# A graph-network layer on one core: node features loaded first in three transfers per 2048 nodes, and the stores of h on GpSimd's queue

## The chip, the core and the metric

The kernel runs on one core of a Trainium2 chip. A core has a matrix engine (TensorE, PE in the profile), a vector engine (VectorE, DVE), a scalar engine (ScalarE, ACT), GpSimd (POOL) and a small engine that issues transfers (SyncE, SP). Each engine works through its own list of instructions in order; semaphores order the engines among each other. Transfers (DMAs) are issued by SP, ACT or POOL and are carried out by 16 DMA engines that all three share. In the profile SPq and ACTq are the issuing side of SP and ACT, and POOLq that of GpSimd; transfers issued by SP and ACT show up under "hardware_dynamic" queues, GpSimd's under "software_dynamic".

The metric is device time in microseconds (us). The kernel before takes 4074.11 us (median of 10 runs, 4069.6 to 4077.16).

## The reference

12,500 nodes with 160 features each (64 scalars and 32 vectors of 3), 400,000 edges sorted by their destination. What matters here, with the constant factors left out:

```
s = x[:, :64];  v = x[:, 64:].reshape(n, 32, 3);  a = node_attr
h_s = s @ lin1_ws * a                      # the table h: 12500 x 160
h_v = einsum('nci,cd->ndi', v, lin1_wv) * a
w   = silu(edge_scalars @ fc_w1) @ fc_w2   # 224 weights for each edge, in five parts w1..w5
es, ev = h_s[edge_src], h_v[edge_src]      # one row of h gathered for each edge
m_s1 = w1 * es * e0;   m_s2 = w4 * (ev . e1);   m_v1 = w2 * es x e1
m_v2 = w3 * ev * e0;   m_v3 = w5 * cross(ev, e1)
agg_s, agg_v = segment_sum(..., edge_dst)
out = layernorm(x + gate(self_connection(x) + agg @ lin2))
```

## The kernel before

**The opening (lines 98 to 396).** Everything from line 95 to line 396 is kept in the order in which it is written, on each engine. It has to leave three things behind: the table h in memory (`h_tab`, 12,500 rows of 640 bytes), a small integer for each edge (`rel`: its destination less the base of its block of three tiles), and the scaled weights.

The table is made in pieces of 2048 nodes (CH, six of them, and a rest of 212). For each piece SP loads the features channel by channel: `xa` (128 x 2048: 64 scalars and the first two components of the 32 vectors) in four transfers (lines 274 and 275, 1024 nodes each), and `xz` (the third component, the piece cut in four quarters that lie under each other, 128 x 512) in four (line 279). All seven pieces have buffers of their own (`nodes`, bufs = 7), so that no load waits for a buffer. PE multiplies 16 tiles of 128 nodes by `l1` (line 316) and the four of `xz` by the block-diagonal `l1z` (line 331). DVE scales the results by the node attribute while it moves them from PSUM to `ht` (lines 319 and 334, five instructions of 128 x 512 for each piece). `ht` has three buffers. ACT then stores the piece (line 345, 128 partitions x 16 rows of 640 bytes, 2048 rows in all), and the rest as one tile of 128 rows and one of 84 (line 348).

Before that, SP loads `rows`, the first destination of each block, straight from `dst` in three transfers of single elements (lines 254 and 255); `bases()` (line 292, called ahead of the fourth piece) turns it into `lo`, the bases spread over 128 partitions, and the flag `early`. After the pieces SP loads the first indices (`idx`), edge attributes (`eat`), edge scalars (`es`, line 228, two halves of 64 x 1536), `w1` and, in ten transfers, `w2` with its columns rearranged (line 289); ACT loads `dt`, all destinations (line 351, 128 x 3125 integers), behind the stores. DVE then scales `w2`, makes `rel` from `dt` and `lo` (lines 387 and 392, 17 instructions) and scales the second layer's weights `l2` (line 111), which SP loads in 20 small transfers (line 380).

**The loop over the edges (from line 785).** 782 steps of four tiles of 128 edges. A step gathers with four indirect transfers on GpSimd's queue (line 427, 128 rows of h each; `hg` has four buffers of four tiles, so GpSimd can be 16 gathers ahead), makes the edge weights on PE (lines 418 and 440), the products of both on DVE (lines 450 and 458, which read `hg`), a selection matrix from `rel` on DVE (lines 504 and 507), sums tiles into blocks on PE (line 514), and adds blocks into an accumulator. The nodes that are complete are finished along the way.

**How transfers are counted.** The framework gives each transfer one of eight semaphores in turn. SP and ACT share one set of eight; GpSimd has eight of its own. A transfer is only issued once the earlier transfer on its semaphore has landed, so that a load on SP can wait for a store that ACT issued.

Of the kernel before, what the change touches and what calls it, by code (L numbers as in the profile page):

```python
# [10 lines left out]
F32 = mybir.dt.float32  # L11
# [9 lines left out]
P = 128  # L21
S = 64
V = 32
# [5 lines left out]
BT = 3  # L29
# [3 lines left out]
KB = 4  # L33
# [7 lines left out]
NWT = 224  # L41
# [12 lines left out]
def gnn_kernel(  # L54
# [21 lines left out]
    nc = tc.nc  # L76
    N = x.shape[0]
    NT = attr.shape[1]
# [4 lines left out]
    NB = -(-TT // BT)  # L83
# [3 lines left out]
    consts = ctx.enter_context(tc.tile_pool(name="consts", bufs=1))  # L87
    dram = ctx.enter_context(tc.tile_pool(name="dram", bufs=1, space=bass.MemoryType.DRAM))
    h_tab = dram.tile([N, D], F32, name="h_tab")
# [5 lines left out]
    in_order = ctx.enter_context(ExitStack())  # L95
    in_order.enter_context(tc.manual_schedule(
        engines={ENG.PE, ENG.DVE, ENG.Activation, ENG.Pool, ENG.SP}))
    at = consts.tile([P, NT], F32, name="at")
    nc.scalar.dma_start(at, attr)

    l1 = consts.tile([P, P], F32, name="l1")
    nc.vector.memset(l1, 0.0)
    nc.scalar.dma_start(l1[:S, :S], lin1_ws)
    for i in range(2):
        r = slice(S + i * V, S + (i + 1) * V)
        nc.scalar.dma_start(l1[r, r], lin1_wv)
    scales = [(l1[:S], 1.0 / math.sqrt(S)), (l1[S:], 1.0 / math.sqrt(V))]

    def scale():
        for m, by in scales:  # L110
            nc.vector.tensor_scalar_mul(m, m, by)
        scales.clear()

    def block_diagonal(name, w, n, scale, queue=nc.scalar):
        k = w.shape[0]
        m = consts.tile([n * k, n * k], F32, name=name)
        nc.vector.memset(m, 0.0)
        for i in range(n):
            queue.dma_start(m[i * k:(i + 1) * k, i * k:(i + 1) * k], w)
        if scale != 1.0:  # L120
            scales.append((m, scale))
        return m

    l1z = block_diagonal("l1z", lin1_wv, 4, 1.0 / math.sqrt(V))
    for m, by in scales:
        nc.scalar.mul(m, m, by)
    scales.clear()


    rel = consts.tile([P, TT], I16, name="rel")  # L130
    rows = consts.tile([1, NB], I32, name="rows")
    early = consts.tile([1, 1], F32, name="early")
# [8 lines left out]
    ends_pool = ends.enter_context(tc.tile_pool(name="ends", bufs=1))  # L141
# [49 lines left out]
    def index(t):  # L191
        a0, idx, _ = ahead(t)
        return idx[:, t - a0:t - a0 + 1]
# [20 lines left out]
    def in_pairs(a):  # L214

        return a.rearrange("o (c k h) -> o h c k", k=KB, h=2)

    ess = {}

    def load_chunk(c):  # L220
        if c in ess:
            return
        t0, halves = chunks[c]
        es = ess[c] = loads.tile([2 * S, SIDE * P], F32, name="es")
        for half, n in enumerate(halves):
            to = es[half * S:(half + 1) * S]
            e0 = (t0 + half * halves[0]) * P
            nc.sync.dma_start(to[:, :n * P], es_t[:, e0:e0 + n * P])


    ident = consts.tile([P, P], F32, name="ident")
# [16 lines left out]
                   base=0, channel_multiplier=0)  # L248
    nc.gpsimd.iota(share[:, even:], pattern=[[RATE, NB - even]], base=even * RATE, channel_multiplier=0)

    with nc.allow_non_contiguous_dma(reason="the first destination of each block"):
        firsts = dst[0:1, 0:(even - 1) * BT + 1:BT].rearrange("o (c h k) -> o h c k", k=KB, h=2)
        for half in range(2):
            nc.sync.dma_start(in_pairs(rows[:, :even])[:, half], firsts[:, half])
        nc.sync.dma_start(rows[:, even:], dst[0:1, even * BT:(NB - 1) * BT + 1:BT])


    U = 4
    dt = ends_pool.tile([P, TT], I32, name="dt")
    lo = ends_pool.tile([P, NB], F32, name="lo")  # L260
# [2 lines left out]
    with tc.tile_pool(name="nodes", bufs=len(starts)) as nodes, tc.tile_pool(  # L263
        name="nodes_ps", bufs=6, space=PSUM
    ) as nps, tc.tile_pool(name="z_ps", bufs=2, space=PSUM) as zps:
        loaded = []
        for c0 in starts:
            cn = min(CH, N - c0)
            quarters = 4 if cn == CH else 1
            assert quarters == 4 or cn <= U * P  # L270
            xa = nodes.tile([P, CH], F32, name="xa")
            for b0 in range(0, cn, CH // 2):
                b1 = min(b0 + CH // 2, cn)
                nc.sync.dma_start(xa[:S, b0:b1], xs_t[:, c0 + b0:c0 + b1])
                nc.sync.dma_start(xa[S:, b0:b1], xv_t[:2 * V, c0 + b0:c0 + b1])
            xz = nodes.tile([P, U * P], F32, name="xz")
            cq = cn // quarters
            for q in range(quarters):
                nc.sync.dma_start(xz[q * V:(q + 1) * V, :cq],
                                  xv_t[2 * V:, c0 + q * cq:c0 + (q + 1) * cq])  # L280
            loaded.append((c0, cn, quarters, cq, xa, xz))
        index(0)
        load_chunk(0)
        for half in range(2):
            r = slice(half * S, (half + 1) * S)
            nc.sync.dma_start(w1[r, r], fc_w1)
            at_c = 0
            for a, b in ((64, 128), (0, 64), (192, 224), (160, 192), (128, 160)):
                nc.sync.dma_start(w2[r, half, at_c:at_c + b - a], fc_w2[:, a:b])
                at_c += b - a  # L290

        def bases():

            base_f = ends_pool.tile([1, NB], F32, name="base_f")
            nc.vector.tensor_copy(base_f, rows)
            for b0 in range(0, NB, U * P):
                b1 = min(NB, b0 + U * P)
                ps = nps.tile([P, U, P], F32, name="hp").rearrange("p u c -> p (u c)")
                nc.tensor.matmul(ps[:, :b1 - b0], ones, base_f[:, b0:b1], start=True, stop=True)
                nc.scalar.copy(lo[:, b0:b1], ps[:, :b1 - b0])  # L300
            nc.vector.tensor_sub(share, rows, share)
            nc.vector.tensor_reduce(early, share, AX.X, OP.min)
            nc.vector.tensor_scalar(early, early, -float(MARGIN), None, op0=OP.is_lt)

        for c0, cn, quarters, cq, xa, xz in loaded:
            if c0 == 3 * CH:
                bases()
            ht = nodes.tile([P, 4 * U, D], F32, name="ht", bufs=3)
            nt = -(-cn // P)
            first = c0 // P  # L310
            full = cn // P
            for t0 in range(0, nt, U):
                ps = nps.tile([P, U, P], F32, name="hp")
                for t in range(t0, min(t0 + U, nt)):
                    n = min(P, cn - t * P)
                    nc.tensor.matmul(ps[:n, t - t0], xa[:, t * P:t * P + n], l1,
                                     start=True, stop=True)
                k = min(U, full - t0)
                nc.vector.tensor_mul(
                    ht[:, t0:t0 + k, :P], ps[:, :k],  # L320
                    at[:, first + t0:first + t0 + k, None].to_broadcast([P, k, P]))
                if t0 + k < nt <= t0 + U:
                    n = cn - full * P
                    nc.vector.tensor_scalar(ht[:n, full, :P], ps[:n, full - t0],
                                            at[:n, first + full:first + full + 1], None, op0=OP.mult)

            pz = zps.tile([P, U, 4, V], F32, name="pz")
            k = quarters * V
            for u in range(-(-cq // P)):
                n = min(P, cq - u * P)  # L330
                nc.tensor.matmul(pz[:n, u, :quarters].rearrange("p q c -> p (q c)"),
                                 xz[:k, u * P:u * P + n], l1z[:k, :k], start=True, stop=True)
            if quarters == 4:
                nc.vector.tensor_mul(
                    ht[:, :, P:].rearrange("p (q u) c -> p u q c", q=4), pz,
                    at[:, first:first + 4 * U].rearrange("p (q u) -> p u q", q=4)[:, :, :, None]
                    .to_broadcast([P, U, 4, V]))
            else:
                nc.vector.tensor_mul(ht[:, :full, P:], pz[:, :full, 0],
                                     at[:, first:first + full, None].to_broadcast([P, full, V]))  # L340
            if cn > full * P:
                n = cn - full * P
                nc.vector.tensor_scalar(ht[:n, full, P:], pz[:n, full, 0],
                                        at[:n, first + full:first + full + 1], None, op0=OP.mult)
            nc.scalar.dma_start(
                h_tab[c0:c0 + full * P, :].rearrange("(q p) d -> p q d", p=P), ht[:, :full])
            if cn > full * P:
                nc.scalar.dma_start(h_tab[c0 + full * P:c0 + cn, :], ht[:n, full])


    nc.scalar.dma_start(dt, dst)
    iota = consts.tile([P, W], F32, name="iota")
    nc.vector.tensor_copy(iota, iota_i)
    nc.vector.tensor_scalar_mul(w2, w2, 1.0 / math.sqrt(64))

    scs = consts.tile([S, V3], F32, name="scs")
    nc.sync.dma_start(scs, sc_ws)
# [606 lines left out]
```

## Time and profile before

| | |
|---|---|
| median of 10 runs | 4074.11 us (4069.6 to 4077.16) |
| the profiled execution, its own time | 4064.87 us |
| its span (first to last instruction) | 4063.1 us |
| PE busy | 3692.2 us, 91% |
| POOL busy | 3007.1 us, 74% |
| DVE busy | 2432.4 us, 60% |
| ACT busy | 939.0 us, 23% |
| bytes moved | 411.77 MB, mean 101 GB/s; 209 GB/s in the first of 40 slices |

The profiled execution lies 9.2 us (0.2%) below the median of the runs. The span is what the trace covers; the remaining 1.8 us lie around it. Busy counts the time in which an engine executes: issuing a transfer is not counted on SP and ACT, but GpSimd's part in an indirect transfer is (line 427). Matmuls are pipelined, so that a PE at 91% is not known to be at its limit. In what follows a line of the timeline reads: start, duration, engine, line of the kernel, operation, output <- input, count, and in brackets the idle time of the engine before it with what ended it ("issue" is a wait that the profile does not explain).

### The profile page before, as it was taken

Reading aid. Unit: us, or ns where it says so; the run is one execution under the profiler, and the core shown is the slowest. Engines: PE = TensorE matmul, PEld = TensorE weight load, DVE = VectorE, ACT = ScalarE, POOL = GpSimd, SP = SyncE. Lnnn points to the kernel's source line nnn. Section 1 sums busy time; section 2 is a strip of 40 time slices with the busy share of each in tenths; the row PEclk is TensorE's granted clock in tenths of the full one; section 3 lists DMA queues with packets and bytes.
Section 4 is the critical chain, followed back from the end, with each engine's and each line's share of the span. In section 5 each row is a group of like instructions: output and inputs, shape, how many; then the busy total and the mean of one; then the engine's idle time right before and its main releaser. Section 6 shows DMA issues by size and latency. Waiting matters only on the chain. (4 is left out here: it accounts for less than half of the span.)

```text
span 4063.1 us, 47627 instructions
## 1 busy us (share of the span) xinstructions
PE 3692.2 (91%) x14291; PEld 1600.9 (39%) x14291; DVE 2432.4 (60%) x6374; ACT 939.0 (23%) x2463; POOL 3007.1 (74%) x3134
## 2 busy tenths in 40 slices
PE   5999998998999989998998989999998999998997
PEld 4343343443433433433433434334343333333443
DVE  4665665665656656656656556565665655655655
ACT  0322221221222222212212122122221221221222
POOL 2777777777777777777777777777777777777775
PEclk7999999999999999999999999999999999999998
DMA  7434444434434434434444344444443443443432
GB/s 209 115 91 101 101 97 102 101 95 104 100 91 108 100 90 108 103 92 107 98 100 100 94 97 108 96 98 103 98 105 94 101 104 94 101 101 97 99 95 57
DMA packets 241211, 411.77 MB, mean 101 GB/s; under 512 B 74200, under 2 KB 171876, under 8 KB 240820
## 3 DMA queue, kind: packets, MB, share of 16 engines
q0 software_dynamic: 150000, 256.20, 26.2%
q1 hardware_dynamic: 77666, 142.75, 14.7%
q10 hardware_dynamic: 13282, 9.69, 0.8%
q8 instruction: 119, 1.95, 0.2%
q14 instruction: 144, 1.18, 0.1%
HBM read 392.40 MB, written 16.00 MB: 101 GB/s over the span
## 5 line engine op out<-in xcount | busy, mean ns | idle before, releaser
L427 POOL DMA_INDIRECT hg<-h_tab,idx x3125 | 3002.3, 961 | 1023.3 <-issue 935.9
L440 PE MATMUL pw<-w,hid 128*128 128x448 f32 x3126 | 1383.9, 567 | 199.9 <-DVE oh L504 191.8
L450 DVE TENSOR_TENSOR pr<-pw,hg 128x512 f32<-128x512 f32 x782 | 539.6, 690 | 1471.0 <-DMA hg<-h_tab,idx 1020.5
L514 PE MATMUL pa<-pr,sel 128*64 128x416 f32 x6250 | 1305.0, 539 | 0.0
L458 DVE TENSOR_TENSOR pr<-pw,hg 128x384 f32<-128x384 f32 x2346 | 1153.5, 546 | 0.1
L440 PEld LDWEIGHTS pw<-w,hid 128*128 128x128 f32 x3126 | 561.0, 196 | 691.8 <-issue 624.8
L514 PEld LDWEIGHTS pa<-pr,sel 128*64 128x64 f32 x6250 | 388.2, 139 | 817.0 <-issue 699.5
L706 ACT COPY sa<-pa 128x416 f32<-128x416 f32 x521 | 263.1, 505 | 1474.0 <-PE pa L514 1471.3
L418 PE MATMUL ph<-es,w 128*128 128x512 f32 (+1 forms) x784 | 453.0, 660 | 16.8 <-DMA w<-in_fc_w_dram 11.7
L420 ACT ACTIVATE hid<-ph 128x512 f32<-128x512 f32 x392 | 233.5, 596 | 734.4 <-PE ph L418 733.9
L523 PEld LDWEIGHTS pt<-ident,sa 128*128 128x128 f32 x2084 | 239.9, 141 | 312.1 <-issue 255.0
L507 DVE TENSOR_TENSOR sel<-oh,eas 128x256 f32<-128x256 f32 x782 | 336.9, 431 | 42.8
L538 PE MATMUL po<-tt,l 128*96 128x256 f32 (+5 forms) x1496 | 346.6, 379 | 4.0 <-DVE z L573 2.6
L523 PE MATMUL pt<-ident,sa 128*128 128x128 f32 x2084 | 328.3, 280 | 2.9 <-DVE acc L687 2.5
L538 PEld LDWEIGHTS po<-tt,l 128*96 128x96 f32 (+1 forms) x1496 | 227.8, 163 | 143.2 <-issue 74.0
L526 ACT COPY tt<-pt 128x192 f32<-128x192 f32 x521 | 164.5, 316 | 506.2 <-PE pt L523 505.7
L418 PEld LDWEIGHTS ph<-es,w 128*128 128x128 f32 x784 | 119.7, 192 | 285.0 <-issue 227.2
L546 DVE TENSOR_TENSOR acc<-acc,os 96x32 f32 x1042 | 193.7, 186 | 24.6 <-ACT os L541 5.4
L504 DVE TENSOR_TENSOR oh<-rel,iota 128x64 f32<-128x64 int16 x782 | 169.5, 217 | 0.1
L572 PE MATMUL pp<-ident,acc 96*128 96x96 f32 x196 | 36.6, 273 | 93.6 <-DVE acc L546 73.4
L528 ACT COPY tt<-pt 128x64 f32<-128x64 f32 x521 | 117.1, 225 | 0.0
L541 ACT COPY os<-po 96x512 f32<-96x512 f32 (+2 forms) x68 | 38.3, 563 | 308.4 <-PE po L538 292.3
(77 smaller groups left out, 630.6 us busy)
## 6 DMA issues: line engine op xcount, KB each, us to landing
es<-in_es_t_dram SPq DMA_DIRECT2D x260, 384.0 KB
hg<-h_tab,idx POOLq DMA_INDIRECT x3125
h_tab<-ht ACTq DMA_DIRECT2D x6, 1280.0 KB
xt<-in_x_dram SPq DMA_DIRECT2D x23, 320.0 KB
out_dram<-y SPq DMA_DIRECT2D x23, 320.0 KB
xv<-in_xv_t_dram SPq DMA_DIRECT2D x25, 187.5 KB
xs<-in_xs_t_dram SPq DMA_DIRECT2D x25, 125.0 KB
xa<-in_xs_t_dram SPq DMA_DIRECT2D x12, 256.0 KB
```

What stands on the lines that cost most here:

```text
L418: nc.tensor.matmul(ph[:k, c], w1[:k, :k], es[:k, t0 * P + c0 * P:t0 * P + c1 * P], start=True, stop=True)
L420: nc.scalar.activation(hid[:k, c], ph[:k, c], AF.Silu, scale=1.0 / math.sqrt(64))
L427: nc.gpsimd.indirect_dma_start(out=hg[:, t, :], out_offset=None, in_=h_tab, in_offset=bass.IndirectOffsetOnAxis(ap=i, axis=0))
L440: nc.tensor.matmul(pw[:, t:t + m, :NWT], hid[:m * S, c * P:(c + 1) * P], w2[:m * S, :m], start=True, stop=True)
L450: nc.vector.tensor_mul(two, pw[:, :n, :2 * S].rearrange("p t (k c) -> p t k c", k=2), hg[:, :n, None, :S].to_broadcast([P, n, 2, S]))
L458: nc.vector.tensor_mul(pr[:, :n, first:first + V3].rearrange("p t (i c) -> p t i c", i=3), pw[:, :n, None, 2 * S + k * V:2 * S + (k + 1) * ...
L507: nc.vector.tensor_mul(sel[:, :n], oh[:, :, None, :].to_broadcast([P, n, 4, W]), by_slot(tiles[0][0])[:, u:u + n, :, None].to_broadcast([P ...
L514: nc.tensor.matmul(pa[half * ROWS:(half + 1) * ROWS, :NPR], sel[:, t].rearrange("p k w -> p (k w)"), pr, start=start, stop=stop)
L523: nc.tensor.transpose(pt[:, four * P:four * P + k], sa[:k, c:c + P], ident[:k, :k])
L538: nc.tensor.matmul(po[:, k, :nb], l2[r, terms[to, part, four]], a[:, :nb], start=(n == 0), stop=(n == len(of) - 1))
L546: nc.vector.tensor_add(window, window, os[:, :, b])
L706: nc.scalar.copy(sa, pas.pop(j)[:, :NPR])
```

## The change

SP's first instructions are now the loads of the first piece; a piece takes three transfers (`xs`, `xv`, and all four quarters of `xz` in one, with the rows in the order channel by quarter, so that `l1z` is filled with a step of four partitions). The first destinations come from one row of `dst` that ACT loads into the first partition of `dt`, from where DVE copies `rows` (three copies in `bases()`). The stores of h, the first two halves of edge scalars and the destinations `dt` are issued by GpSimd, in this order, ahead of the first gather; the store of the last 84 rows goes to SP. `fc_w2` is loaded whole in two transfers (`raw`), and DVE rearranges it while it scales it (ten instructions for one).

```diff
-    with nc.allow_non_contiguous_dma(reason="the first destination of each block"):
-        firsts = dst[0:1, 0:(even - 1) * BT + 1:BT].rearrange("o (c h k) -> o h c k", k=KB, h=2)
-        for half in range(2):
-            nc.sync.dma_start(in_pairs(rows[:, :even])[:, half], firsts[:, half])
-        nc.sync.dma_start(rows[:, even:], dst[0:1, even * BT:(NB - 1) * BT + 1:BT])
...
-        for c0 in starts:
+        def load(c0):
...
-            for b0 in range(0, cn, CH // 2):
-                b1 = min(b0 + CH // 2, cn)
-                nc.sync.dma_start(xa[:S, b0:b1], xs_t[:, c0 + b0:c0 + b1])
-                nc.sync.dma_start(xa[S:, b0:b1], xv_t[:2 * V, c0 + b0:c0 + b1])
+            nc.sync.dma_start(xa[:S, :cn], xs_t[:, c0:c0 + cn])
+            nc.sync.dma_start(xa[S:, :cn], xv_t[:2 * V, c0:c0 + cn])
             xz = nodes.tile([P, U * P], F32, name="xz")
             cq = cn // quarters
-            for q in range(quarters):
-                nc.sync.dma_start(xz[q * V:(q + 1) * V, :cq],
-                                  xv_t[2 * V:, c0 + q * cq:c0 + (q + 1) * cq])
+            z = xv_t[2 * V:, c0:c0 + cq]
+            if quarters == 4:
+                nc.sync.dma_start(xz[:, :cq], bass.AP(tensor=z.tensor, offset=z.offset,
+                                                      ap=[[z.ap[0][0], V], [cq, 4], [1, cq]]))
+            else:
+                nc.sync.dma_start(xz[S:S + V, :cq], z)
...
+        load(starts[0])
+        at = consts.tile([P, NT], F32, name="at")
+        nc.scalar.dma_start(at, attr)
...
+        l1z = consts.tile([P, P], F32, name="l1z")
+        nc.vector.memset(l1z, 0.0)
+        for q in range(4):
+            nc.scalar.dma_start(l1z[q:q + 4 * V - 3:4, q * V:(q + 1) * V], lin1_wv)
...
+        nc.scalar.dma_start(dt[0:1], dst[0:1])
+        for c0 in starts[1:]:
+            load(c0)
         index(0)
-        load_chunk(0)
+        raw = ends_pool.tile([2 * S, NWT], F32, name="raw")
         for half in range(2):
             r = slice(half * S, (half + 1) * S)
             nc.sync.dma_start(w1[r, r], fc_w1)
-            at_c = 0
-            for a, b in ((64, 128), (0, 64), (192, 224), (160, 192), (128, 160)):
-                nc.sync.dma_start(w2[r, half, at_c:at_c + b - a], fc_w2[:, a:b])
-                at_c += b - a
+            nc.sync.dma_start(raw[r], fc_w2)
 
         def bases():
 
+            firsts = dt[0:1, 0:(even - 1) * BT + 1:BT].rearrange("o (c h k) -> o h c k", k=KB, h=2)
+            for half in range(2):
+                nc.vector.tensor_copy(in_pairs(rows[:, :even])[:, half], firsts[:, half])
+            nc.vector.tensor_copy(rows[:, even:], dt[0:1, even * BT:(NB - 1) * BT + 1:BT])
...
-            nc.scalar.dma_start(
+            nc.gpsimd.dma_start(
                 h_tab[c0:c0 + full * P, :].rearrange("(q p) d -> p q d", p=P), ht[:, :full])
             if cn > full * P:
-                nc.scalar.dma_start(h_tab[c0 + full * P:c0 + cn, :], ht[:n, full])
-
-
-    nc.scalar.dma_start(dt, dst)
+                nc.sync.dma_start(h_tab[c0 + full * P:c0 + cn, :], ht[:n, full])
+
+
+    load_chunk(0, nc.gpsimd)
+    nc.gpsimd.dma_start(dt, dst)
...
-    nc.vector.tensor_scalar_mul(w2, w2, 1.0 / math.sqrt(64))
+    for half in range(2):
+        r = slice(half * S, (half + 1) * S)
+        at_c = 0
+        for a, b in ((64, 128), (0, 64), (192, 224), (160, 192), (128, 160)):
+            nc.vector.tensor_scalar_mul(w2[r, half, at_c:at_c + b - a], raw[r, a:b], 1.0 / math.sqrt(64))
+            at_c += b - a
```

The definitions of `at`, `l1`, `scale` and `block_diagonal` move behind `load(starts[0])` unchanged; `load_chunk` gets its queue as an argument. In the order of instructions of the changed program two things move with it: SP issues the store of the last 84 rows behind five loads of the edge loop (`xs`, `xv` of the self-connection, `idx`, `eat`), and the 20 scalings of `l2` on DVE, which in the program before lie between the products of the first three steps, come ahead of the first product.

More of the change, by code (lines that the diff above doesn't have):

```diff
@@ L97, in gnn_kernel @@
         engines={ENG.PE, ENG.DVE, ENG.Activation, ENG.Pool, ENG.SP}))
[L98 to L127, printed above, removed]
     rel = consts.tile([P, TT], I16, name="rel")
@@ L218, in gnn_kernel, with load_chunk @@
     ess = {}
-    def load_chunk(c):
+    def load_chunk(c, queue=nc.sync):
         if c in ess:
@@ L227, in load_chunk @@
             e0 = (t0 + half * halves[0]) * P
-            nc.sync.dma_start(to[:, :n * P], es_t[:, e0:e0 + n * P])
+            queue.dma_start(to[:, :n * P], es_t[:, e0:e0 + n * P])
     ident = consts.tile([P, P], F32, name="ident")
@@ new lines, in gnn_kernel, with scale @@
+        nc.scalar.dma_start(at, attr)
+        l1 = consts.tile([P, P], F32, name="l1")
+        nc.vector.memset(l1, 0.0)
+        nc.scalar.dma_start(l1[:S, :S], lin1_ws)
+        for i in range(2):
+            r = slice(S + i * V, S + (i + 1) * V)
+            nc.scalar.dma_start(l1[r, r], lin1_wv)
+        scales = [(l1[:S], 1.0 / math.sqrt(S)), (l1[S:], 1.0 / math.sqrt(V))]
+        def scale():
+            for m, by in scales:
+                nc.vector.tensor_scalar_mul(m, m, by)
+            scales.clear()
@@ new lines, in block_diagonal @@
+        def block_diagonal(name, w, n, scale, queue=nc.scalar):
+            k = w.shape[0]
+            m = consts.tile([n * k, n * k], F32, name=name)
+            nc.vector.memset(m, 0.0)
+            for i in range(n):
+                queue.dma_start(m[i * k:(i + 1) * k, i * k:(i + 1) * k], w)
+            if scale != 1.0:
+                scales.append((m, scale))
+            return m
+        l1z = consts.tile([P, P], F32, name="l1z")
+        nc.vector.memset(l1z, 0.0)
+        for q in range(4):
+            nc.scalar.dma_start(l1z[q:q + 4 * V - 3:4, q * V:(q + 1) * V], lin1_wv)
@@ L282, in gnn_kernel @@
+        scales.append((l1z, 1.0 / math.sqrt(V)))
+        for m, by in scales:
+            nc.scalar.mul(m, m, by)
+        scales.clear()
+        nc.scalar.dma_start(dt[0:1], dst[0:1])
+        for c0 in starts[1:]:
+            load(c0)
         index(0)
-        load_chunk(0)
+        raw = ends_pool.tile([2 * S, NWT], F32, name="raw")
         for half in range(2):
@@ L327, in gnn_kernel @@
             pz = zps.tile([P, U, 4, V], F32, name="pz")
-            k = quarters * V
+            r = slice(0, P) if quarters == 4 else slice(S, S + V)
+            by = l1z if quarters == 4 else l1[r, r]
             for u in range(-(-cq // P)):
@@ L331, in gnn_kernel @@
                 nc.tensor.matmul(pz[:n, u, :quarters].rearrange("p q c -> p (q c)"),
-                                 xz[:k, u * P:u * P + n], l1z[:k, :k], start=True, stop=True)
+                                 xz[r, u * P:u * P + n], by, start=True, stop=True)
             if quarters == 4:
```

## The prediction

> **What bounds the kernel now.** I read the shares of busy time first, then the waits of the costliest line, then the opening in order of time, and the rates of the DMA engines last. PE leads by busy time (91%), but GpSimd's gathers never pause. All instructions of line 427 with the idle time before them:
>
> ```profile
> L427 POOL DMA_INDIRECT hg<-h_tab,idx x3125: 942/946/1785, 77.1 to 4030.1; - x196
> ...
>   issue: 935.9, 2838
> ```
>
> 3125 gathers run from 77.12 us to 4031.0, so one each 1.265 us: 0.961 busy (3002.3/3125) and 0.30 before it. The waits on other work that the same view lists (DMA 23.8 us in 78 times, DVE 22.6 in 74) are these same 0.30 us each. After the last gather 32.1 us are left (4063.1 - 4031.0). Hence, as long as the loop's first products keep up,
>
> span = T + 3953.9 + 32.1, with T the start of the first gather, now 77.12.
>
> PE doesn't set the pace: in every 500 us of the loop it is busy 458 to 465 us, some 8% of slack. The chain of waits reaches back only 23 us from the end and says nothing on this. So the change is worth what it does to T. The opening (lines of the timeline):
>
> ```profile
> 0.75 1.98 SPq L254 DMA_DIRECT2D rows<-in_dst_dram  x2
> ...
> 6.51 0.64 SPq L255 DMA_DIRECT2D rows<-in_dst_dram  x1
> ...
> 7.19 0.53 SPq L274 DMA_DIRECT2D xa<-in_xs_t_dram  x1
> ...
> 11.88 5.17 PE L316 MATMUL hp<-l,xa 128*128 128x128 f32 x32 [11.88 <-DMA xa<-in_xv_t_dram]
> ...
> 18.71 20.72 ACTq L345 DMA_DIRECT2D h_tab<-ht  x3
> ...
> 73.28 0.94 ACTq L351 DMA_DIRECT2D dt<-in_dst_dram  x1
> ...
> 77.12 1.13 POOL L427 DMA_INDIRECT hg<-h_tab,idx  x1 [71.76 <-issue]
> ```
>
> The first feature load leaves only at 7.19, the first piece of h is ready at 18.7, and the first gather waits for the last store. What SP waits for in the first 200 us:
>
> ```profile
> SPq L274 <- DMA h_tab<-ht: 22.5, 3, 7.9
> ...
> SPq L289 <- DMA h_tab<-ht: 8.0, 1, 8.0
> ...
> SPq L255 <- DMA rows<-in_dst_dram: 3.8, 1, 3.8
> ```
>
> Loads wait for stores although they share no data: they share semaphores. The DMA engines, in stretches of 5 us (the last two numbers are their busy share and GB/s):
>
> ```profile
> 10.00:15.00 5.00, 3.12 (x16) 3.15 (x17) 0.69 (x1) 0.00 (x0) 0.00 (x0) 1.00 1.04 242
> ...
> 25.00:30.00 5.00, 0.00 (x0) 0.00 (x0) 0.54 (x1) 0.00 (x0) 0.00 (x0) 0.84 1.15 342
> ...
> 45.00:50.00 5.00, 4.93 (x42) 4.74 (x41) 3.48 (x6) 0.00 (x0) 0.00 (x0) 0.95 0.66 159
> ```
>
> Loads alone move at 242 GB/s, stores, alone or mixed with loads, at up to 342, and in between there are holes. DMA is nearly full from 10 to 75 us, so this is the floor that any reordering meets.
>
> **The change part by part.**
>
> *Loads first.* The three transfers for `rows` leave SP: the first load goes out at 0.75 instead of 7.19. Its piece (1.05 MB in `xa`) needs 4.3 us at 242 GB/s plus some 1.5 us of latency, so is there at about 7. ACT's weights are then later: the third fill of `l1z` waits on the semaphore of the first `xs` load, ACT's table load (1.28) and three scalings (0.31 each) stand behind it, so PE starts at about 9.4 instead of 11.88. From PE's start to a complete piece took 6.8 us (11.88 to 18.68): first piece at 16.
>
> *Fewer loads.* Six pieces at eight transfers of 0.4 to 0.6 us become 18 transfers; SP's issuing was not the limit, but its 22.5 us of waits for stores go, because stores no longer use the hardware semaphores. What is late next is the DMA engines themselves.
>
> *Bases from a row.* Three copies on DVE ahead of line 295 (0.68 us for 1042 integers): some 0.8 us, hidden in DVE's waits of 39.7 us for PE in the opening; without this cover 0.8 us. ACT's load of one row replaces nothing that anyone waits for before the fourth piece.
>
> *w2.* Eight transfers fewer on SP, ten scalings instead of one of 0.41: ten by about 0.175 (median of the 20 scalings of line 111) is 1.75 us, under the wait for the stores; uncovered, 1.3 us. It removes a wait: DVE sat 13.06 us until the last of `w2` had landed, and `rel` only started behind it at 84.0.
>
> *Stores on GpSimd.* This decides. In front of the first gather GpSimd now issues six stores of 2048 rows, one of 128, two of `es` (64 rows each) and `dt` (128). The trace has one kind of transfer that GpSimd issues, the gather of 128 rows, 0.95 us plus 0.30. If a transfer costs GpSimd the same whatever its rows, a store takes 0.95; if it costs by rows, 16 times as much, 15.1. Neither end is excluded. A part of the 0.95 must be paid once (reading the indices, reporting the end), and a direct store reads no indices: with half of it fixed a store takes 0.47 + 16 x 0.47 = 8.0, with three quarters fixed 0.71 + 16 x 0.24 = 4.5. I take 6, the middle of these two. With e for a store's time on GpSimd, T by GpSimd = 16 + 6(e + 0.3) + 5.3; the 5.3 are the four small transfers at 1.25, and the last store lands (1.31 MB at 311 to 342 GB/s, about 4 us, and some latency) in that time. e = 0.95 gives 28.8, e = 6 gives 59.1, e = 8 gives 71.1, e = 15.1 gives 113.7. It is worse than now from e = 9.0 on.
>
> The Trainium skill, "DMA: Bandwidth & Descriptors", section Anatomy of one DMA, calls the generation of descriptors small and says that many can be emitted before a cost shows; no run here shows it yet. By it e lies near 1, and T is set by the DMA engines.
>
> *The DMA floor.* 8.0 MB of features, 8.0 of stores and 0.9 of indices, attributes and weights go before T. Loads alone from 2 us until the first store is emitted (16 + 6 = 22) are 20 us x 242 GB/s = 4.8 MB; the other 12.1 MB at 311 (the mean from 50 to 57 us) to 342 GB/s take 35 to 39 us: 57 to 61. With 1.5 us to land and report, T = 59 to 62. With e = 0.95 the same sum gives 57 to 61. Taking both limits, T = 61.
>
> Against this floor speaks a rule of the same page (Rules for kernel authors): spreading transfers over SP, ACT and GpSimd brings no bandwidth, as all run on the same DMA engines. By that rule the stretch moves its bytes as before and gains only the earlier start: 77.1 - 6.4 = 70.7. The rows of this trace, 242 GB/s with one queue and 342 with two, speak for the mix.
>
> *`es` and `dt` on GpSimd, and DVE's new order.* Both lie in GpSimd's queue behind the stores, 2.4 MB at 342 GB/s: `dt` is there about 7 us after T. The gathers' data follow it. On DVE 17 `rel` instructions (6.65 us, 84.0 to 90.6), 21 scalings (about 4 us; SP issues their 24 transfers in 11 us behind the store of 84 rows, which waits for DVE's last piece) and the first products (0.67 + 3 x 0.56 = 2.4) come next: T + 7 + 13 = T + 20. The 17th gather, which needs the first `hg` back, is due 21.7 us after the first (98.82 - 77.12). So nothing stalls, with 1.6 us to spare; I add 1 us for it.
>
> Sum: T 77.1 to 61 is -16.1, stall +1: span 4048, against 4063.1. The profiled execution lay 9.2 us under the median, so the same difference from 4074.1: **4059 us**.
>
> **The rivals.**
>
> *GpSimd pays by the row (slower).* Its place is the queue in front of the first gather. At e = 15.1, T = 113.7, +36.6: 4111 us; it decides from e = 9.0 on, and is over 0.2% (8.1 us) from e = 10.4. For it: 946 ns, with a minimum of 942, for each 128 rows is as constant as a loop over rows. Against: line 427 has to fetch 128 indices, a store has none.
>
> *The transfers are the bound.* T = 70.7: 4068 us. For it: a busy share of 0.9 to 1.15 from 10 to 45 us; against: 242 against 342 GB/s.
>
> *The start of the loop takes over.* T is early, but `dt` shares its way with gathers and small loads. From 80 to 85 us now 105 GB/s are moved; if `es` and `dt` (2.4 MB) go at some 115, they are there at T + 21, the first products end at T + 34, and the gathers wait 12 us: 4059 + 11 = 4070. Against it: `dt` moved at over 300 GB/s from 73 to 79 us, beside the first gathers.
>
> *The change doesn't do what it says*, if loads still waited for stores. In the changed order SP's loads wait only for loads and ACT's small transfers, so I give it nothing.
>
> **How the numbers follow.** Forecast (T of 54 to 68) 0.55, paying by the row 0.25, transfers 0.10, start of the loop 0.10. What a measurement of this kernel can tell from no change is about 0.2%, 8 us. Faster by more takes T under 69, so e under 7.6: the forecast and a little of the transfers, 0.57. Within: the two middle rivals and e from 7.6 to 10.4, 0.17. Slower: the rest, 0.26. The likeliest one's own range is 4050 to 4066. The whole range starts there too (T = 53 at the best rates) and reaches to e = 12.3 (T = 97, +20) at the top: 4050 to 4094.
>
> **What would show it.** Right: first load before 1 us, first piece by 17, GpSimd's stores of about 6 us each, a first gather near 61, gathers every 1.265 us from there on. Wrong: stores of over 9 us on GpSimd; a first gather on time but pauses over 0.30 us after the 16th; a DMA rate that stays at 240 with stores in flight; gathers slower than 1.265 us in the loop, which no part of the change touches.

## The result and the profile after

| | before | after |
|---|---|---|
| median | 4073.86 us (28 runs, 4069.21 to 4077.49) | 4053.09 us (8 runs, 4045.29 to 4058.69) |
| ratio, 95% interval | | 0.9948 [0.9940, 0.9957] |
| profiled execution, its span | 4063.1 us | 4048.3 us |
| T, start of the first gather | 77.12 us | 68.71 us |
| first gather to end of the last | 3953.9 us | 3948.3 us |
| after the last gather | 32.1 us | 31.3 us |

The change takes 20.8 us off the median, 15 were predicted. The span fell by 14.8, of which T is 8.4, the gathers 5.6 and the end 0.8. The predicted terms were 16.1 for T and a loss of 1 in the loop.

The view of the costliest line after (operation; shortest, median and longest duration in ns; first and last start; then what ended the idle time before it, in us and times):

```profile
L438 POOL DMA_INDIRECT hg<-h_tab,idx x3125: 942/946/1618, 68.7 to 4016.1; - x196
...
  issue: 864.8, 2839
...
  DMA l<-in_lin_ws_dram: 13.5, 1
```

The median gather is the same, 946 ns, and no pause between two gathers is longer than 0.316 us: nothing stalls once the loop runs. What is new is one wait of 13.5 us ahead of the first gather. Here is the opening, as lines of the timeline:

```profile
0.76 0.58 SPq L235 DMA_DIRECT2D xa<-in_xs_t_dram  x1
...
2.94 0.54 ACTq L253 DMA_DIRECT2D l<-in_lin_ws_dram  x1
...
8.35 0.60 SPq L241 DMA_DIRECT2D xz<-in_xv_t_dram  x1
...
10.26 5.79 PE L320 MATMUL hp<-l,xa 128*128 128x128 f32 x32 [10.26 <-ACT l L280]
...
17.99 1.39 POOL L350 DMA_DIRECT2D h_tab<-ht  x1 [12.62 <-DVE ht L339]
...
50.73 1.15 POOL L350 DMA_DIRECT2D h_tab<-ht  x1 [3.32 <-DVE ht L339]
...
52.97 0.57 POOL L350 DMA_DIRECT2D h_tab<-ht  x1 [1.09 <-DVE ht L348]
...
53.41 0.99 SPq L353 DMA_DIRECT2D h_tab<-ht  x1
...
54.59 0.58 POOL L357 DMA_DIRECT2D dt<-in_dst_dram  x1
...
68.71 1.04 POOL L438 DMA_INDIRECT hg<-h_tab,idx  x1 [13.55 <-DMA l<-in_lin_ws_dram]
...
68.99 3.21 DVE L398 TENSOR_TENSOR rel<-dt,lo 128x260 int16<-128x260 int32 x6 [12.99 <-DMA dt<-in_dst_dram]
```

A store of 2048 rows costs GpSimd 1.15 to 1.39 us, one of 128 rows 0.57. GpSimd has issued everything by 55.2 and then sits idle for 13.55 us. Its stores of h are not what it waits for: by their semaphores in the trace the last of them landed at 60.7. The store of the last 84 rows, which the change gave to SP, left at 53.4 and landed at 67.8, 0.95 us before the first gather. In every profile of this document the first gather starts 0.91 to 1.07 us after the last store of h has landed. The view names another DMA (`l<-in_lin_ws`), which uses the same semaphore as the first load of `idx`, for which the gather waits too. But of GpSimd's waiting instructions in the trace those for its own last stores end at 60.69 and that for the 84 rows at 67.79, and the experiments confirm that it was this store.

SP's waits after, in the same stretch (what was waited for: us in total, times, longest):

```profile
SPq L235 <- DMA xa<-in_xv_t_dram: 6.6, 3, 3.2
SPq L241 <- DMA l<-in_lin_ws_dram: 6.4, 1, 6.4
...
SPq L391 <- DMA h_tab<-ht: 2.9, 1, 2.9
```

The feature loads no longer wait for stores, which had cost 22.5 us. In their place stands a new wait: the third load of the first piece stands at 8.35 behind ACT's first weight. The rates of the DMA engines (last two numbers: busy share and GB/s):

```profile
5.00:10.00 5.00, 0.00 (x0) 0.00 (x0) 0.00 (x0) 1.69 (x3) 0.36 (x2) 1.00 0.48 85
10.00:15.00 5.00, 4.74 (x25) 4.74 (x25) 1.38 (x2) 0.52 (x2) 0.00 (x0) 1.00 1.03 250
...
20.00:25.00 5.00, 3.98 (x36) 3.82 (x35) 2.78 (x5) 0.00 (x0) 1.19 (x1) 1.00 1.05 231
...
35.00:40.00 5.00, 5.00 (x33) 5.00 (x32) 2.16 (x4) 0.00 (x0) 0.00 (x0) 0.67 1.06 385
...
65.00:70.00 5.00, 2.05 (x2) 0.50 (x2) 1.01 (x2) 1.68 (x2) 1.04 (x1) 0.50 0.47 177
```

Half of 5 to 10 us is a hole, left by that wait. The feature loads alone still move at 225 to 250 GB/s, though their runs in memory are now 8 KB and not 4; from 25 to 55 us, with stores moving beside them, the sum is 341 to 385. The first store was issued at 17.99, but in the window of 20 to 25 us only SP's queue moves bytes: the first packet of the store goes at 25.07, 7.1 us after its issue. (Before, with ACT issuing, it was 2.6 us, 18.71 to 21.29.) What fills this time is not in the profile. From 65 to 70 us the engines are half idle in the mean; up to 67 they are still full. So bytes alone don't tell why a store of 53 KB takes until 67.8. What it shared the engines with shows in the packets of each queue (packets, MB, share of the 16 engines) from 64 to 66 us:

```profile
q0 software_dynamic: 62, 0.78, 93.4%
q1 hardware_dynamic: 62, 0.01, 3.0%
```

and from 67 to 68 us:

```profile
q0 software_dynamic: 17, 0.06, 16.2%
q1 hardware_dynamic: 171, 0.03, 15.3%
```

While `dt` runs on GpSimd's queue in packets of 12.5 KB, SP's queue gets one small packet through for each of them, 62 and 62. Once `dt` is through, 171 pass in half the time. The 84 rows lie on SP behind five loads of the edge loop, issued from 47.8 to 52.4. Their own 84 packets of 640 bytes start between 58.9 and 66.8, beside `es` and `dt` (packets of 6 and 12.5 KB). These 2 us also show that a load can be fast alone: `dt` made nearly all of the 0.79 MB, 393 GB/s. What holds the feature loads at 225 to 250 was not tested.

### The profile page after: what moved, and what is told of

Same layout as the page of the kernel before. It is cut to its first block, busy times and chain, and to the rows that moved or that the text cites. A ratio compares the mean times of both kernels' runs of the same rounds, so it can differ in the third digit from the quotient of the medians.

```text
span 4048.3 us, 47586 instructions
## 1 busy us (share of the span) xinstructions
PE 3686.4 (91%) x14291; PEld 1593.9 (39%) x14291; DVE 2433.9 (60%) x6386; ACT 938.4 (23%) x2463; POOL 3010.9 (74%) x3144
## 5 line engine op out<-in xcount | busy, mean ns | idle before, releaser
L438 POOL DMA_INDIRECT hg<-h_tab,idx x3125 | 2996.6, 959 | 965.2 <-issue 864.8
```

The lines of the kernel that those rows point to most:

```text
L438: nc.gpsimd.indirect_dma_start(out=hg[:, t, :], out_offset=None, in_=h_tab, in_offset=bass.IndirectOffsetOnAxis(ap=i, axis=0))
```

## The experiments

My theory (A): the mechanism of the prediction holds, both parts of the change count, and T stands at 68.7 and not at 61 only because the store of 84 rows lies on SP. Rivals: that the bytes before T set it anyway (the prediction's "transfers are the bound"), that one part alone does everything, that an earlier T is lost again at the start of the loop, and, for the first piece, that it is late for the loads or for the weights. The kernels ran in three groups, each on one chip with its own runs of the kernel before, and ratios are to those. Before took 4065.98 us in the first group (21 runs; the first four sections below), 4082.36 in the second (9 runs; the next three), 5116.11 in the third (25 runs; the last section).

### The last 84 rows on GpSimd

```diff
-                nc.sync.dma_start(h_tab[c0 + full * P:c0 + cn, :], ht[:n, full])
+                nc.gpsimd.dma_start(h_tab[c0 + full * P:c0 + cn, :], ht[:n, full])
```

> The changed kernel with the store of the last 84 rows of h on GpSimd's queue, behind the 128-row store, instead of on SP's. Theory A: in the changed kernel the first gather (68.7 us) waits for this one store alone, which SP issues at 53.4 us and which lands at 68.4 to 68.8, while GpSimd's own stores have landed by 61; then the first gather starts at 61 to 62, the span falls by about 7 us and the median from 4053 to about 4046. Theory B: the first gather waits until the DMA engines have moved everything that was issued, whatever the queue; then it starts at 68 to 69 as before and the median stays at 4053. Theory C: it starts at 61, but rel, which waits for dt until 69.0, and the first products come no earlier; the 17th gather is then due at 61 + 21.7 = 82.7 with the first products ending at 82.1, so GpSimd pauses for 0 to 2 us and most of the gain stays.

Measured: 4042.31 us, ratio 0.9943 [0.9930, 0.9957]. The timeline of this kernel:

```profile
53.35 0.57 POOL L353 DMA_DIRECT2D h_tab<-ht  x1
...
61.53 1.04 POOL L438 DMA_INDIRECT hg<-h_tab,idx  x1 [5.99 <-DMA h_tab<-ht]
...
68.92 6.35 DVE L398 TENSOR_TENSOR rel<-dt,lo 128x260 int16<-128x260 int32 x12 [13.34 <-DMA dt<-in_dst_dram]
```

One word moves T from 68.7 to 61.5, with the same bytes in front of it. That speaks for A and against T = 70.7, the "transfers are the bound": at T = 61.5 the engines were at a share of 1.00 to 1.06 in every 5 us from 10 us on, so this is about the floor that they allow with this mix of transfers. The longest pause later in the loop is 0.32 us, so nothing of it is lost again. The time says less: the ratio is hardly below the 0.9948 of the change, which was measured elsewhere. The second group has both side by side.

### The old queues

The loads of the changed kernel, with all stores of h and `dt` on ACT, and the first edge scalars on SP:

```diff
         index(0)
+        load_chunk(0)
...
-            nc.gpsimd.dma_start(
+            nc.scalar.dma_start(
...
-                nc.sync.dma_start(h_tab[c0 + full * P:c0 + cn, :], ht[:n, full])
+                nc.scalar.dma_start(h_tab[c0 + full * P:c0 + cn, :], ht[:n, full])
...
-    load_chunk(0, nc.gpsimd)
-    nc.gpsimd.dma_start(dt, dst)
+    nc.scalar.dma_start(dt, dst)
```

> The changed kernel with the stores of h and dt back on ACT's queue and the first es on SP's; loads first in three transfers, the row of bases and the single load of fc_w2 stay. Theory A (the shared semaphores cost the time): SP's loads wait for stores again, some 20 us in all; the first gather gains only the earlier start, 77.1 - 6 = 71 or later; median 4066 to 4072. Theory B (the earlier start and the fewer transfers are the change, the queue is not): first gather at 69 or earlier, median 4053.

Measured: 4059.15 us, ratio 0.9984 [0.9975, 0.9993], T 70.44, just under the 71 that A gives as the least. The time lies under A's range because before was faster on this chip too. What SP waits for in this kernel:

```profile
SPq L235 <- DMA h_tab<-ht: 12.6, 1, 12.6
SPq L153 <- DMA h_tab<-ht: 7.9, 1, 7.9
SPq L241 <- DMA l<-in_lin_ws_dram: 6.4, 1, 6.4
...
SPq L196 <- DMA h_tab<-ht: 3.0, 1, 3.0
...
SPq L241 <- DMA h_tab<-ht: 2.5, 1, 2.5
```

Loads first, with the fewer transfers, the row of destinations and the whole `fc_w2`, are worth 6.7 us of T by themselves. The loads wait for stores as they did before, 26.0 us in all (12.6 + 7.9 + 3.0 + 2.5; before 22.5 + 8.0), because SP and ACT share their semaphores again.

### Stores on GpSimd alone

The kernel before, with nothing moved but the queue of the stores and of `dt`:

```diff
-            nc.scalar.dma_start(
+            nc.gpsimd.dma_start(
...
-                nc.scalar.dma_start(h_tab[c0 + full * P:c0 + cn, :], ht[:n, full])
+                nc.gpsimd.dma_start(h_tab[c0 + full * P:c0 + cn, :], ht[:n, full])
...
-    nc.scalar.dma_start(dt, dst)
+    nc.gpsimd.dma_start(dt, dst)
```

> The kernel before with the stores of h (the last 84 rows too) and dt on GpSimd's queue and nothing else changed: loads still in eight transfers for each piece, behind the three for rows. Theory A: without the shared semaphores loads and stores overlap at 340 to 380 GB/s instead of taking turns; first gather at 64 to 67 (61 and the later start of the loads, 6.4 us, less the 2.5 us in which the changed kernel's SP waits for ACT's weights); median 4060 to 4064. Theory B: the first gather stays at 75 to 77, median 4071 to 4074. The SP waits of loads for stores are 0 by both.

Measured: 4055.72 us, ratio 0.9975 [0.9966, 0.9985]. The median is lower than expected since this chip's kernel before was too; T is what was expected:

```profile
20.01 1.39 POOL L345 DMA_DIRECT2D h_tab<-ht  x1 [14.63 <-DVE ht L334]
...
66.48 1.03 POOL L427 DMA_INDIRECT hg<-h_tab,idx  x1 [6.84 <-DMA h_tab<-ht]
```

No load on SP waits for a store in this kernel. The queue alone takes 10.6 us off T, more than loads first; together, with all stores on GpSimd, they take 15.6 (77.1 - 61.5), less than the sum of 17.3.

### The kernel before, a second profile

> The kernel before once more, for a second profile: how far the duration of the 3125 gathers (3953.9 us from first to last in the profile before, 3948.3 in the one after) and the first gather differ between executions of the same kernel. If the 5.6 us are chance, it shows a value between 3948 and 3962; the first gather should be at 77 within 1 us.

Measured: 4067.4 us in its one execution, T 77.71, the gathers 3954.4, the rest 33.4. T and the gathers repeat to 0.6 us.

### The changed kernel and the version above, again

> The changed kernel as it is, on the same chip as the next one, so that the two medians can be held against each other. First gather at 68.7 within 0.5 us, again released when the store of 84 rows on SP's queue lands; median 12 to 21 us under the kernel before.

> The changed kernel with the last 84 rows stored by GpSimd, once more. Theory A (that store alone held the first gather): first gather at 61.5, median 7 us (5 to 9) under the changed kernel's of the same call. Theory B (the lower median of the first run was the chip): within 3 us of it.

Measured: 4059.42 us, 0.9943 [0.9929, 0.9956], T 69.2 for the change; 4050.55 us, 0.9924 [0.9911, 0.9938], T 62.4 with the 84 rows on GpSimd. The medians differ by 8.9 us and T by 6.8. The gathers of the changed kernel took 3012.3 us in this profile, against 2996.6 in the first one. So the 5.6 us by which they were shorter after than before lie within the scatter between executions of one kernel, and can't be put down to the change.

### Weights earlier

The version above, with the zero fills of `w2` and `l2` moved behind ACT's load of the row of destinations, so that the fill of `l1` comes first on DVE:

```diff
-    w2 = consts.tile([2 * S, 2, NWT], F32, name="w2")
-    nc.vector.memset(w2, 0.0)
-    l2 = consts.tile([P, 11, V3], F32, name="l2")
-    nc.vector.memset(l2, 0.0)
...
         nc.scalar.dma_start(dt[0:1], dst[0:1])
+        w2 = consts.tile([2 * S, 2, NWT], F32, name="w2")
+        nc.vector.memset(w2, 0.0)
+        l2 = consts.tile([P, 11, V3], F32, name="l2")
+        nc.vector.memset(l2, 0.0)
```

> As the run before, and the zero fills of w2 and l2 on DVE (0.43 and 0.94 us) behind those of l1 and l1z. In the changed kernel ACT issues the first weight at 2.94 because the fill of l1 stands behind them, and SP's third load waits for that weight until 8.35 while the DMA engines run empty. Theory A (the late issue costs it): the third load leaves at 6.8 to 7.2 and the first gather at 60 to 60.5. Theory B (the weight's small packets lie behind the 8 KB packets of the first load, whenever it is issued): the third load leaves at 8 and the first gather stays at 61.5. Median 0 to 2 us under the run before; this is under what a run can tell, so the profile decides.

Measured: 4049.68 us, 0.9924 [0.9910, 0.9937], T 61.1. From its timeline:

```profile
1.36 0.56 ACTq L249 DMA_DIRECT2D l<-in_lin_ws_dram  x1
...
8.30 0.60 SPq L237 DMA_DIRECT2D xz<-in_xv_t_dram  x1
8.92 5.68 PE L320 MATMUL hp<-l,xa 128*128 128x128 f32 x32 [8.92 <-DMA l1z<-in_lin_wv_dram]
```

The weights leave 1.6 us earlier (1.36, not 2.94) and PE starts 1.3 earlier than in the change, but SP's third load still goes at 8.30. It waits for the landing of a weight that travels beside two large loads, and not for its issue. T gains 1.3 against the run beside it, the median 0.9, within its scatter.

### Weights on GpSimd

The version just shown, with the loads of `l1` and `l1z` (seven, not six as the expectation has it) on GpSimd's queue, so that SP shares no semaphore with them. The two iotas of `share` move behind them on GpSimd (not shown):

```diff
-        nc.scalar.dma_start(l1[:S, :S], lin1_ws)
+        nc.gpsimd.dma_start(l1[:S, :S], lin1_ws)
...
-            nc.scalar.dma_start(l1[r, r], lin1_wv)
+            nc.gpsimd.dma_start(l1[r, r], lin1_wv)
...
-            nc.scalar.dma_start(l1z[q:q + 4 * V - 3:4, q * V:(q + 1) * V], lin1_wv)
+            nc.gpsimd.dma_start(l1z[q:q + 4 * V - 3:4, q * V:(q + 1) * V], lin1_wv)
```

> As the run before, and the six loads of l1 and l1z on GpSimd's queue (ahead of the iota of share), so that none of SP's loads shares a semaphore with them. SP's loads then wait for loads alone and the DMA engines do not run empty between 6 and 9 us. Theory A (the opening is set by bytes moved): first gather at 58.5 to 59.5, median 2 to 3 us under the run with only the 84 rows moved. Theory B (the weights land later behind more load packets, PE starts at 12 or later instead of 10.3, and the first store with it): first gather at 61 or later, no gain.

Measured: 4055.91 us, 0.9940 [0.9926, 0.9953], T 62.0. A window of this kernel, two lines of its timeline, and one of SP's waits:

```profile
5.00:10.00 5.00, 0.00 (x0) 0.00 (x0) 0.00 (x0) 1.33 (x2) 4.54 (x4) 1.00 1.05 228
```

```profile
14.36 0.31 ACT L272 ACTIVATE l1z<-l1z 128x128 f32<-128x128 f32 x1 [3.33 <-DMA l1z<-in_lin_wv_dram]
...
19.25 1.24 POOL L350 DMA_DIRECT2D h_tab<-ht  x1 [9.71 <-DVE ht L339]
```

```profile
SPq L227 <- DMA dt<-in_dst_dram: 7.6, 1, 7.6
```

The hole is gone (share 1.05, not 0.48), and nothing is won. With the engines full of loads, the last weights land later (`l1z` is scaled at 14.36; 9.29 in the version before), and the first store leaves at 19.25 instead of 16.54. The wait that looked like a loss had held the way open for the weights. That this is why T doesn't fall is argued and not shown: SP still shared semaphores with ACT's row of destinations, which ACT issues behind the weights, and waited 7.6 us for it, though the engines stayed full meanwhile (a share of 0.9 to 1.2 from 14 to 24 us). Its median is 5 to 6 us above the two runs beside it although T is not; what makes it so was not found.

### Backlog or big packets

Two kernels ask what holds the 84 rows on SP. The first issues them on ACT, whose queue is empty by then:

```diff
-                nc.sync.dma_start(h_tab[c0 + full * P:c0 + cn, :], ht[:n, full])
+                nc.scalar.dma_start(h_tab[c0 + full * P:c0 + cn, :], ht[:n, full])
```

> The changed kernel, with the store of the last 84 rows issued by ACT instead of SP. In the profile of the changed kernel this store is issued on SP at 53.4 us behind five loads of the edge loop and lands at 68.7, while all of GpSimd's stores have landed by 60.9. Theory A (the store is late because it lies behind SP's five loads in SP's own queue, whose small packets take turns with the 12.5 KB packets of dt): ACT's queue is empty at that point, 84 packets on 16 engines are about 5 on each, so even with a big packet of about 0.7 us between any two of them it lands some 4 to 6 us after its issue, by 60. GpSimd's last store then decides: T 61 to 63, and the time is 6 to 8 us under the changed kernel of the same call. Theory B (any transfer that another engine issues beside GpSimd's big ones is held until those are through, whatever lies before it in its own queue): it still lands at 66 or later, T 67 to 70, and the time is that of the changed kernel within 3 us.

The second leaves them on SP and takes the big packets from GpSimd's queue:

```diff
-    load_chunk(0, nc.gpsimd)
-    nc.gpsimd.dma_start(dt, dst)
+    load_chunk(0)
+    nc.sync.dma_start(dt, dst)
```

> The changed kernel, with the first two halves of edge scalars and the destinations dt issued by SP, behind the store of the last 84 rows, instead of GpSimd. SP's five loads still lie before that store, but GpSimd's queue carries only the stores of h, in packets of 640 bytes. Theory A (backlog on SP, made long by taking turns with big packets): with the big packets gone the five loads and the store are through by about 61, so T is 61 to 63 and the time 6 to 8 us under the changed kernel; dt leaves SP at about 55 and lands at about 68 to 71, so rel starts about where it did and no gather waits longer than 0.3 us. Theory C (the backlog of five loads alone holds the store, big packets or not): the store still lands at 66 or later, T 67 to 70, and dt behind it lands at 75 or later.

The changed kernel ran beside them:

> The changed kernel a third time, beside the other two of this call, as their measure. Both theories: T 68 to 70 and a ratio to the kernel before of 0.993 to 0.996. Open is only the sum by which the gathers are longer than 946 ns each: it was 43 us and 59 us in the two profiles of this kernel so far, and a third value says whether these are two states or a scatter.

Measured: 5111.15 us, 0.9998 [0.9973, 1.0022] with the rows on ACT; 5116.03, 1.0001 [0.9971, 1.0030] with the big transfers on SP; 5115.16, 0.9998 [0.9965, 1.0031] for the change. This chip ran all kernels, that before too, a quarter slower, with a granted clock of 0.88 where the profile of before has 0.96. The times therefore decide nothing between the theories, and all three expectations of time failed. T can still be read. The changed kernel first, by who waited for the store of 84 rows:

```profile
L353 SPq DMA_DIRECT2D h_tab<-ht x1: 749/749/749, 53.0 to 53.0; - x1
...
who waited for it (us, times):
  POOL hg L438: 10.6, 1
```

Here the profile puts the wait of the first gather down to that store. T is 65.32, below the 68 to 70 expected. The other two, first the rows on ACT, then the big transfers on SP:

```profile
53.36 0.33 ACTq L353 DMA_DIRECT2D h_tab<-ht  x1
...
62.36 1.04 POOL L438 DMA_INDIRECT hg<-h_tab,idx  x1 [6.70 <-issue]
```

```profile
53.64 0.61 SPq L353 DMA_DIRECT2D h_tab<-ht  x1
...
62.69 1.03 POOL L438 DMA_INDIRECT hg<-h_tab,idx  x1 [9.78 <-issue]
```

Either remedy brings T to the 61 to 63 that A expects, from a store issued at the same 53 us. So neither SP's backlog by itself nor the big packets by themselves hold it: it takes a queue with a backlog that has to alternate with big packets. The packets in the traces show the way: from ACT's empty queue the 84 rows go between 56.2 and 59.5 us, on SP ahead of the big transfers between 57.9 and 59.9, and in both kernels T is then set by GpSimd's own last store (landed at 61.3 and 61.7). In the changed kernel on this chip they go between 58.8 and 63.0 and land at 64.4, behind all of GpSimd's stores (60.2). The difference on this chip is 2.6 to 3.0 us against one profile of the change, where it was 7 elsewhere; the direction is shown, the size less surely.

What became of the earlier T on this chip shows in the view of the gathers of the changed kernel there:

```profile
L438 POOL DMA_INDIRECT hg<-h_tab,idx x3125: 940/946/1815, 65.3 to 5074.2; - x196
...
  DVE oh L515: 1035.5, 237
  issue: 902.1, 2800
```

The gathers are as fast as ever, but wait 1036 us for DVE, which hands buffers of `hg` back late. GpSimd no longer sets the pace, so the sum "T plus a fixed time for the gathers" doesn't hold, and no gain is seen; the interval would still allow one of 0.35%. Why DVE is late is not shown. A matmul of line 451 takes 608 ns there, 565 in the first profile of the change, but PE's busy time is only 288 us longer (3974.4 against 3686.4) and the span 1068 us, and PE was busy 78% of it. DVE's products (line 461) wait 478 us for PE and 1267 us for something that the profile doesn't name.

## Why the prediction was right, and where it was not

*What bounds the kernel: right, on chips with a granted clock near 0.96.* From T on the gathers ran without a pause over 0.32 us in every such profile. On the chip that granted 0.88 they waited 1036 us for DVE, and the condition of the sum, that the loop's products keep up, was not met.

*Loads first: right, a size off.* First load at 0.76 as predicted; PE at 10.26 instead of 9.4, the first piece at 17.7 instead of 16. The step "ACT's weights are then later" counted the engine work behind the weights, but not that DVE's zero fill of `l1` now stands behind those of `w2` and `l2` (ACT issues at 2.94). Moving the fills gave PE 1.3 us back. The waits of SP for ACT's small transfers, which the prediction put at nothing, came to 6.4 us; without them T was 62.0, no better than with them.

*Waits for stores: right.* The 22.5 us on the feature loads are gone; with the old queues the loads wait 26.0 us for stores again.

*Stores on GpSimd: the mis-sized term.* The forecast took e = 6 us a store, from bounds of 0.95 and 15.1. It is 1.15 to 1.39 for 2048 rows and 0.57 for 128, so about 0.3 ns a row ((1.15 - 0.57)/1920). The split of the gather into a fixed half and a part by rows was wrong, and the rival "GpSimd pays by the row" falls. The Trainium skill, "DMA: Bandwidth & Descriptors", section Anatomy of one DMA, which calls descriptor generation small, agrees with these busy times. They are not the whole delay of a store, though: the first packet of the first one went 7.1 us after its issue, and the profile doesn't tell why.

*The DMA floor: right, and the reason why T is not there was overlooked.* The sum gave 59 to 62 with e = 6 and 57 to 61 with e = 0.95, and GpSimd's last store landed at 60.7. One of its terms was right by luck: it let loads move alone until 22 us because of e = 6, and they did so until 25.07, though e was 1.4 and the first piece later. The step that failed is "with e for a store's time on GpSimd, T by GpSimd": it counts GpSimd's queue alone. The store of 84 rows was named as something that SP's later loads wait for, and was costed at nothing for T. It cost 7 us (68.7 against 61.5). The rule that the prediction set against the floor (same page, Rules for kernel authors: spreading over issuing engines adds no bandwidth) gave T = 70.7, closer to 68.7, but not for its reason. With the same bytes T went to 61.5, and stores and loads together moved at 341 to 385 GB/s, where the feature loads alone had 225 to 250. This measurement decides here, but it has stores beside loads; no run spreads the same feature loads over two queues.

*The start of the loop: right but for the 1 us.* In the change T is late, so `dt` was there when the first gather started (`rel` at 68.99), and the first products ended at 82.1, T + 13.4. The forecast of T + 7 and T + 20 shows in the version with T = 61.5: `rel` starts at 68.92, T + 7.4, and the first products end at 82.05, T + 20.5, before the 17th gather is due at T + 21.7. So the stall of 1 us that was added did not come in either, and that rival falls.

*The size.* That 20.8 us were measured and 15 predicted is no proof of the sum, and in part luck: T gave half of its term. Of the other 12.4 us, the profiles hold 6.4 (the gathers 5.6, the end 0.8); the remaining 6 are the medians' distance from single profiles, 9.0 us before (4073.86 against 4064.87) and 3.0 after (4053.09 against 4050.12). Gathers that overlap with DVE's work, above all on `sel` and `acc`, take more than the 946 ns, 43 to 59 us in all (in the first profile of the change the 734 with no DVE instruction beside them lose 0.2 us together), and this sum differs by 16 us between two executions of the changed kernel. The old queues and the stores alone gained what T did to 1 us (6.8 us of time for 6.7, 10.3 for 10.6, against the T of 77.12 before). The 84 rows on GpSimd gained 23.7 for 15.6, and on the second group's chip all four versions gained 11 to 17 us more than T (their T against 77.12). Where that surplus is from stays open.

## What to carry to other kernels

When several queues feed one wait, work out the landing of the last transfer on each of them, and look for the smallest one too: a store of 53 KB behind a short backlog, taking turns with packets of up to 12.5 KB, held the kernel back for 7 us. Before filling a hole in the DMA's time, ask which small transfer passes through it. And a gain ahead of a loop lasts only while the same engine sets the pace of that loop: on a chip that granted PE 0.88 nothing of it could be seen.

## What the runs showed of the hardware

- Issuing a direct store of 2048 rows costs GpSimd 1.15 to 1.39 us, of 128 rows 0.57, a gather of 128 rows 0.95. The first packet of the first store of 2048 rows went 4.5 to 7.1 us after its issue on GpSimd, 2.6 us on ACT.
- Two queues with work share an engine packet by packet, not byte by byte: 62 packets with 0.78 MB beside 62 with 0.01 MB from 64 to 66 us.
- Doubling the runs of the feature loads from 4 to 8 KB didn't raise their rate (242 GB/s before, 225 to 250 after). Stores and loads together moved at up to 385 GB/s, `dt` nearly alone at 393.
- One chip ran the same kernels in 5.1 ms instead of 4.04 to 4.08, with a granted clock of 0.88 instead of 0.96. That the clock is the cause is not shown.
